# Ten row tiles of a count moved from a dense stage to a gather stage, two PSUM copies moved to VectorE, stores moved to SyncE

## Chip, cores and metric

The kernel runs on one core of a Trainium2 chip. A core has five engines with a queue of instructions each: TensorE (PE in the profile; its weight loads are PEld), VectorE (DVE), ScalarE (ACT), GpSimd (POOL) and SyncE (SP). Each works through its own queue in order and waits on semaphores for the others. The metric is the device time of one execution in microseconds. Times are medians of several runs.

## Reference

Four graph layers follow one another on `x` of 4096 x 256. Each adds its result to `x`, and each starts from `h = relu(layernorm(x))`. The adjacency matrix `adj` is 4096 x 4096 int32 with zeros and ones, about 0.8% ones.

```python
# layer 0: attention over adj, then a dense part for every row
Wh = h @ W                                    # 256 x 256
h_attn = softmax(where(adj > 0, leaky(e_src + e_dst), -9e15)) @ Wh
h_enh = silu(ln(Wh @ fe1_w + fe1_b)) @ fe2_w + fe2_b
B, C, dt = split(Wh @ W_bcdt + b_bcdt, 3)
hs = Wh * ((softmax(dt + A) * B) @ abp_w + abp_b)
h_part, z = split(hs @ W_hz + b_hz, 2)
hs = ((h_part * silu(z) + h_part * D) @ out_w + out_b) * (1 + C @ cp_w + cp_b)
g = sigmoid(silu(ln(concat(h_attn, hs) @ g1_w + g1_b)) @ g2_w + g2_b)
x = x + ln(g * h_attn + (1 - g) * hs + h_enh)
# layer 1: mean over the neighbours, then a projection
a = (adj == 1); deg = a.sum(axis=1)
x = x + (a @ h / deg) @ W.T + b
# layer 2: attention with a leaky logit, elu at the end
# layer 3: attention with Q K^T logits, adj + identity as mask
```

What the change is about is `deg`, the number of ones of each row, which layer 1 divides by, and the dense part of layer 0.

## The kernel before

Rows are cut into 32 tiles of 128 (`NT`), four tiles make a block (`BT`), and there are 8 blocks (`NB`). Each row of `adj` is cut into four quarters of 1024 columns (`NQ`, `QW`). `x` stays on the core in `xs`.

Layer 0's attention loads `adj` as bf16, turns it on PE, codes it and stores the codes to DRAM (`codesT`) for the later layers. Its results are in `xs` and in the projected rows `wh`.

The dense part of layer 0 follows (lines 561 to 798). `dense(b)` is a generator that works one block through all products and yields 30 times. `turn` (L594) transposes four 128 x 128 parts on PE into a PSUM tile of tag `tp`, of which there are three, and has it copied out by the function given: `onto` is a VectorE copy (L602), `nc.scalar.copy` one on ACT (recorded at L599). It is used for `whT` (two halves k = 0 and 1, L661), for `abT` (L703; it lies in a buffer called `kept`, so the profile writes `kept<-tp`), for `comb` (four parts, L754) and for the two `hidden` stages, where ACT evacuates with Silu (L625). `normed` computes row statistics on DVE, a power on POOL (L116), an offset on DVE (L611), and applies both on ACT (L614).

Beside it run the counts. `count(g)` takes one quarter of one row tile (a `[128, 1024]` bf16 tile `a`, loaded by a casting DMA that POOL issues, L639) and runs two ACT instructions over it (L647): the sign of `a - 0.5` and the sign of `a - 1.5`, each summed along the row into `over[:, t, v, q]`. The difference of the two sums, halved, is the number of ones. There are 32 x 4 = 128 such counts and so 256 sign activations. Four `a` buffers (`AHEAD`) are filled three ahead. `with_counts(b)` puts one count behind each of the first 16 steps of `dense(b)`.

`run_staggered(gens, period)` (L29) takes one step of every active generator per tick and starts a new one every `period` ticks, here 16. So the second half of block b runs beside the first half of block b+1, and every tick has one count until the last block is past its sixteenth step. The order in which the program states instructions is not kept exactly: the framework's scheduler may put a ready instruction of later work ahead in its engine's queue.

Layer 1 (L803 to 868) first reduces `over` to `rdeg`, the reciprocal of the degree, for all 32 tiles at once (L837 to 841). `block1(b)` normalizes a block, transposes it and projects it into `v1` (value and rounding rest, so 512 columns). Then `gather(t)` runs for each row tile:

```python
eq = (code == UNIT)                              # DVE, L852, two buffers
for c in range(NT): acc += eq[:, c].T @ v1[:, c] # PE, L856, 32 products, acc has two buffers
lo = acc[:, D:]                                  # ACT, L862
o = (acc[:, :D] + lo) * rdeg[:, t] + b1          # DVE, L864, L865
xs[:, t] += o                                    # DVE, L866
```

The codes come by DMAs of SP (L847) into four buffers. Layer 2 and layer 3 are attentions that read the codes again. In layer 3 each block of two row tiles ends in `weigh3`, which divides, adds `xs` and stores the rows with a DMA issued by POOL (L1109). SP issues the loads of codes of the following row blocks there (`fetch3`, L1006).

Of the kernel before, what the change touches and what calls it, by code (L numbers as in the profile page):

```python
# [21 lines left out]
P = 128  # L22
# [19 lines left out]
def kernel(ctx: ExitStack, tc: tile.TileContext, w: dict, out: bass.AP):  # L42
    nc = tc.nc
    x, adj = w["x"], w["adj"]
    N, D = x.shape
    NT = N // P
    KD = D // P
    BT = 4
    NB = NT // BT
    BW = BT * P  # L50
    QW = 1024
    NQ = N // QW
# [98 lines left out]
    def products(ps, lhsT_of, rhs_of, n):  # L151
        for k in range(n):
            nc.tensor.matmul(  # L153
                out=ps, lhsT=lhsT_of(k), rhs=rhs_of(k), start=(k == 0), stop=(k == n - 1)
            )

# [183 lines left out]
    with ExitStack() as l0:  # L340
# [10 lines left out]
        with ExitStack() as es:  # L351
# [155 lines left out]
            with ExitStack() as ps_:  # L507
# [53 lines left out]
        wp = l0.enter_context(tc.tile_pool(name="l0_w", bufs=1))  # L561
        with ExitStack() as es:
            d = es.enter_context(tc.tile_pool(name="l0_d", bufs=1))
            AHEAD = 4
            code_p = es.enter_context(tc.tile_pool(name="l0_code", bufs=AHEAD))
            small = es.enter_context(tc.tile_pool(name="l0_s", bufs=4))
            pst = es.enter_context(tc.tile_pool(name="l0_pt", bufs=3, space=PSUM))
# [26 lines left out]
            def turn(dst, parts, take):  # L594

                ps = pst.tile([P, BW], F32, tag="tp", name="tp")
                for i, part in enumerate(parts):
                    nc.tensor.transpose(ps[:, ts(i, P)], part, ident)
                take(dst, ps)  # L599
# [30 lines left out]
                        yield  # L630
                return zT

            asked, came = [(t, q) for t in range(NT) for q in range(NQ)], []

            def ask(n):
                for t, q in asked[len(came) : n]:

                    came.append(code_p.tile([P, QW], BF16, tag="a", name="a", bufs=AHEAD))
                    nc.gpsimd.dma_start(out=came[-1], in_=adj[ts(t, P), ts(q, QW)])  # L639

            def count(g):

                ask(g + AHEAD - 1)
                t, q = asked[g]
                for v in range(2):
                    sign = code_p.tile([P, QW], BF16, tag="sign", name="sign", bufs=1)
                    nc.scalar.activation(  # L647
                        sign, came[g], AF.Sign, bias=limits[:, v : v + 1],
                        accum_out=over[:, t, v, q : q + 1],
                    )  # L650

            def dense(b):
                at = ts(b, BT)
# [3 lines left out]
                    out=xt, in_=x[ts(b, BW), :].rearrange("(t p) d -> p t d", p=P)  # L657
# [3 lines left out]
                for k in range(KD):  # L661
                    turn(
                        whT[:, k, :], [wh[:, b * BT + i, ts(k, P)] for i in range(BT)],
                        onto if k else nc.scalar.copy,
                    )
                yield

# [5 lines left out]
                dt = bc[:, :, S : 2 * S]  # L673
# [26 lines left out]
                        yield  # L700
                yield from normed(t1, "fe")
                abT = parts[1, BW][:, 0, :]
                turn(abT, [dt[:, i, :] for i in range(BT)], nc.scalar.copy)  # L703
                yield
                hsT = parts[KD, BW]
                for k in range(KD):
# [81 lines left out]
                nc.gpsimd.tensor_tensor(f, f, xt, ALU.add)  # L788

            def with_counts(b):  # L790
                at, n = b * BT * NQ, BT * NQ
                for k, _ in enumerate(dense(b)):
                    if k < n:
                        count(at + k)
                    yield

            ask(AHEAD - 2)
            run_staggered([with_counts(b) for b in range(NB)], 16)

    with ExitStack() as es:  # L803
        vp = es.enter_context(tc.tile_pool(name="l1_v", bufs=1))
        v1 = vp.tile([P, NT, 2, D], F32R, name="v1")
        w1 = load_matrix(vp, "L1_gnn_WT")
        b1 = load_row(vp, "L1_gnn_b")
        code_p = es.enter_context(tc.tile_pool(name="l1_code", bufs=4))
        eq_p = es.enter_context(tc.tile_pool(name="l1_eq", bufs=2))
        work = es.enter_context(tc.tile_pool(name="l1_work", bufs=2))  # L810
        small = es.enter_context(tc.tile_pool(name="l1_s", bufs=4))
        pst = es.enter_context(tc.tile_pool(name="l1_pst", bufs=2, space=PSUM))
        psm = es.enter_context(tc.tile_pool(name="l1_psm", bufs=3, space=PSUM))
        ps_acc = es.enter_context(tc.tile_pool(name="l1_acc", bufs=2, space=PSUM))

        def block1(b):
            h = work.tile([P, BT, D], F32, tag="h", name="h")
            preln(small, xs[:, ts(b, BT), :], h)
            yield
            hT = transposed_block(work, pst, h, "hT")  # L820
            yield
            for i in range(0, BT, 2):
                ps = psm.tile([P, 2, D], F32, tag="mm", name="mm")
                for u in range(2):
                    products(
                        ps[:, u, :], lambda k: hT[:, k, ts(i + u, P)], lambda k: w1[:, k, :], KD
                    )
                at = slice(b * BT + i, b * BT + i + 2)
                nc.scalar.copy(v1[:, at, 0, :], ps)
                nc.vector.tensor_tensor(  # L830
                    v1[:, at, 1, :], ps, v1[:, at, 0, :].bitcast(F32), ALU.subtract
                )
                yield


        sums = vp.tile([P, NT, 2], F32, name="sums")
        nc.vector.tensor_reduce(sums, over, AX.X, ALU.add)  # L837
        rdeg = vp.tile([P, NT], F32, name="rdeg")
        nc.vector.tensor_tensor(rdeg, sums[:, :, 0], sums[:, :, 1], ALU.subtract)
        nc.vector.tensor_scalar(rdeg, rdeg, 0.5, None, ALU.mult)  # L840
        nc.vector.reciprocal(rdeg, rdeg)
        run_staggered([block1(b) for b in range(NB)], 2)

        def gather(t):
            code = code_p.tile([P, N], BF16, tag="code", name="code")
            for q in range(NQ):
                nc.sync.dma_start(  # L847
                    out=code[:, ts(q, QW)].rearrange("p (c i) -> p c i", i=P),
                    in_=codesT[t // RB][q][:, t % RB, :, :],
                )  # L850
            eq = eq_p.tile([P, N], F32R, tag="eq", name="eq")
            nc.vector.tensor_scalar(eq, code, UNIT, None, ALU.is_equal)  # L852
            yield
            acc = ps_acc.tile([P, 2 * D], F32, tag="acc", name="acc")
            for c in range(NT):
                nc.tensor.matmul(  # L856
                    out=acc, lhsT=eq[:, ts(c, P)], rhs=v1[:, c, :, :],
                    start=(c == 0), stop=(c == NT - 1),
                )
            yield  # L860
            lo = work.tile([P, D], F32, tag="lo", name="lo")
            nc.scalar.copy(lo, acc[:, D : 2 * D])  # L862
# [72 lines left out]
    with ExitStack() as l3:  # L935
# [59 lines left out]
        code_p = l3.enter_context(tc.tile_pool(name="l3_code", bufs=2))  # L995
# [95 lines left out]
        def weigh3(b):  # L1091
            st = rows3[b]
            accs = [ps_acc.tile([P, D + 1], F32, tag="acc", name="acc") for _ in range(RT)]
            for c in range(NT):
                for r in range(RT):
                    nc.tensor.matmul(  # L1096
                        out=accs[r], lhsT=st["y"][:, r, c, :], rhs=v3[:, c, :],
                        start=(c == 0), stop=(c == NT - 1),
                    )
                yield  # L1100
            for r in range(RT):
                t = b * RT + r
                rden = small.tile([P, 1], F32, tag="rden", name="rden")
                nc.vector.reciprocal(rden, accs[r][:, D : D + 1])  # L1104
                o = work.tile([P, D], F32, tag="o", name="o")
                nc.vector.scalar_tensor_tensor(
                    o, accs[r][:, 0:D], rden, xs[:, t, :], ALU.mult, ALU.add
                )
                nc.gpsimd.dma_start(out=out[ts(t, P), :], in_=o)  # L1109

        fetch3(0)
        signs3(0)
# [51 lines left out]
```

## Time and profile before

| what | value |
| --- | --- |
| median of 3 runs | 3056.92 us (3055.16 to 3063.83) |
| the profiled execution's own time | 3058.37 us |
| span of its record | 3056.6 us |
| PE busy | 2874.6 us, 94% |
| DVE busy | 1854.3 us, 61% |
| ACT busy | 1275.1 us, 42% |
| POOL busy | 965.4 us, 32% |
| sign activations (L647) | 256, 1148 ns mean, 293.9 us |
| reading their sums (L647) | 256, 190 ns mean, 48.6 us |
| products of layer 1's sums (L856) | 1024, 239.3 us |
| stores of the result on POOL (L1109) | 32, 542 ns mean |

In the profile a busy time is the time in which an engine had an instruction running. A group is named by line, engine, operation and `out<-in`; "idle before" is how long the engine stood still just ahead of such instructions, with the releaser that ended the wait. The dense part lies between about 624 and 1221 us of the span, layer 1's projections between 1240 and 1286, its sums from there to about 1521.

### The profile page before, as it was taken

The page shows a single profiled execution, that of the slowest core. Times are in us where ns is not written, and L with a number is a line of the kernel's source. Part 1 is how long each engine was busy: PE and PEld are TensorE (multiplying, and loading weights), DVE is VectorE, ACT ScalarE, POOL GpSimd, SP SyncE. Part 2 cuts the span into 40 slices and gives each one's busy share as a digit, 9 for nine tenths or more (in the row PEclk, how much of TensorE's full clock was granted, in tenths as well). Part 3 has the DMA queues.
Part 4 walks back from the last instruction along what each step waited for, and adds up shares of the span by engine and source line. Part 5 has one row for each costly group of instructions (what it writes and reads, how often), then busy time and mean ns, then how long its engine had stood idle before and what let it go on. Part 6 is the DMA issues. An engine that isn't in the chain of part 4 may idle for free.

```text
span 3056.6 us, 34943 instructions
## 1 busy us (share of the span) xinstructions
PE 2874.6 (94%) x13353; PEld 2341.0 (77%) x13353; DVE 1854.3 (61%) x3304; ACT 1275.1 (42%) x1944; POOL 965.4 (32%) x749
## 2 busy tenths in 40 slices
PE   6989999999899999799969999999999999999998
PEld 5778888866555566588758887888888888888887
DVE  5876767335444453544488887745766566566562
ACT  5766555379999963400054434443212111111111
POOL 4676665534454433100026555550000000000000
PEclk9999999999999999899979999999999999999999
DMA  6966655154444420344222222101101101101000
GB/s 143 212 145 126 139 124 154 39 80 76 74 76 75 76 36 7 102 138 141 81 106 79 90 69 83 56 18 59 63 33 61 39 33 61 38 33 61 33 7 8
DMA packets 105745, 234.94 MB, mean 77 GB/s; under 512 B 10701, under 2 KB 27081, under 8 KB 97385
## 3 DMA queue, kind: packets, MB, share of 16 engines
q0 software_dynamic: 39152, 73.04, 15.7%
q1 hardware_dynamic: 63752, 157.04, 14.9%
q10 hardware_dynamic: 2672, 2.62, 0.3%
q8 instruction: 105, 1.72, 0.2%
q14 instruction: 64, 0.52, 0.1%
HBM read 261.96 MB, written 37.81 MB: 98 GB/s over the span
## 4 chain that ended last, share of the span: by engine, by line
issue 26%; PE 17%; DVE 3%; POOL 2%; DMA 1%; ACT 1%; POOLq 0%; DVEq 0%; ACTq 0%
PE acc L325 11%; PE s L153 3%; PE acc L1096 2%; DVE run L237 1%; PE mm L153 1%; DVE y L283 1%; POOL y L287 1%; DMA turned<-codesT 1%; POOL out_dram L1109 1%; ACT y L314 0%; POOL pl_rs L116 0%; ACT hp L889 0%; PE q_ps L153 0%; ACT h L133 0%; DMA ab_row<-l_ab_d 0%
## 5 line engine op out<-in xcount | busy, mean ns | idle before, releaser
L325 PE MATMUL acc<-v,y 128*128 128x257 f32 x4096 | 935.0, 386 | 36.1 <-ACT hp L889 18.5
L325 PEld LDWEIGHTS acc<-v,y 128*128 128x128 f32 x4096 | 776.3, 193 | 151.6 <-ACT hp L889 23.7
L287 POOL TENSOR_TENSOR y<-y,turned 128x1024 f32<-128x1024 f32 (+1 forms) x272 | 550.1, 2037 | 301.5 <-DVE y L283 261.9
L314 ACT ACTIVATE y<-y,sdst 128x512 f32<-128x512 f32 (+1 forms) x544 | 350.7, 689 | 360.7 <-POOL y L287 360.5
L283 DVE SCALAR_TENSOR_TENSOR y<-ab_row,cdst,b 128x512 f32<-128x512 f32 (+1 forms) x544 | 368.6, 711 | 162.5 <-PE acc L325 103.0
L1096 PE MATMUL acc<-v,y 128*128 128x257 f32 x2048 | 454.5, 380 | 0.4 <-DVE rden L1104 0.4
L153 PE MATMUL s<-qT,hT 128*128 128x256 f32 x2048 | 445.2, 379 | 0.7 <-ACT qT L1044 0.7
L153 PEld LDWEIGHTS s<-qT,hT 128*128 128x128 f32 x2048 | 389.2, 190 | 53.9 <-ACT qT L1044 1.4
L1089 ACT ACTIVATE y<-y 128x1024 f32<-128x1024 f32 x128 | 132.2, 1055 | 714.3 <-DVE y L1088 710.0
L1096 PEld LDWEIGHTS acc<-v,y 128*128 128x128 f32 x2048 | 387.4, 190 | 55.6 <-issue 0.8
L237 DVE SCALAR_TENSOR_TENSOR run<-turned,v,run 128x512 f32<-128x512 bf16 (+1 forms) x527 | 379.8, 721 | 58.3 <-DMA turned<-codesT 28.0
L1109 POOL DMA_DIRECT2D out_dram<-o x32 | 17.3, 542 | 933.7 <-DVE rden L1104 932.9
L647 ACT ACTIVATE sign<-a,limits 128x1024 bf16<-128x1024 bf16 x256 | 293.9, 1148 | 18.5 <-DMA a<-in_adj_dram 12.9
L856 PE MATMUL acc<-v,eq 128*128 128x512 f32 x1024 | 239.3, 395 | 0.0
L1058 DVE SCALAR_TENSOR_TENSOR y<-code,s 128x512 f32<-128x512 bf16 x256 | 175.9, 688 | 100.4 <-PE s L153 100.1
L856 PEld LDWEIGHTS acc<-v,eq 128*128 128x128 f32 x1024 | 192.7, 189 | 44.8 <-DVE eq L852 0.3
L1088 DVE TENSOR_TENSOR y<-y,top 128x1024 f32<-128x1024 f32 x128 | 146.2, 1216 | 43.0 <-PE top L1082 43.0
L1065 DVE TENSOR_TENSOR mx<-mx,y 128x512 f32<-128x512 f32 x224 | 154.9, 691 | 7.4
L407 ACT ACTIVATE turned<-cT,log_wide 128x1024 bf16<-128x1024 bf16 x128 | 140.9, 1101 | 32.8 <-PE cT L402 32.5
L153 PE MATMUL mm<-kept 128*128 128x512 f32 x288 | 139.4, 620 | 10.1 <-ACT kept L599 8.6
L852 DVE TENSOR_SCALAR eq<-code 128x4096 fp32r<-128x4096 bf16 x32 | 73.4, 2293 | 114.8 <-PE acc L856 114.8
L153 PE MATMUL mm<-kept,zT 128*128 128x256 f32 x512 | 116.8, 381 | 0.0
(214 smaller groups left out, 2744.0 us busy)
## 6 DMA issues: line engine op xcount, KB each, us to landing
adj_t<-in_adj_dram POOLq DMA_DIRECT2D x128, 256.0 KB, 4.6
codesT<-turned SPq DMA_DIRECT2D x32, 1024.0 KB
a<-in_adj_dram POOLq DMA_DIRECT2D x128, 256.0 KB, 4.2
code<-codesT SPq DMA_DIRECT2D x128, 256.0 KB
turned<-codesT SPq DMA_DIRECT2D x32, 1024.0 KB
code<-codesT SPq DMA_DIRECT2D x64, 512.0 KB
ab_row<-l_ab_d SPq DMA_DIRECT2D x15, 512.0 KB
xt<-in_x_dram SPq DMA_DIRECT2D x8, 512.0 KB
```

Source lines behind the costliest of these rows:

```text
L153: nc.tensor.matmul(out=ps, lhsT=lhsT_of(k), rhs=rhs_of(k), start=(k == 0), stop=(k == n - 1))
L237: nc.vector.scalar_tensor_tensor(st["run"], code, dst, st["run"], ALU.subtract, ALU.min)
L283: nc.vector.scalar_tensor_tensor(y[:, :, k, :], st["ab"][:, 0, :, :], self.cdst[:, c + k : c + k + 1], st["b"], ALU.add, ALU.max,)
L287: nc.gpsimd.tensor_tensor(y, y, mask[:, :, c % QT : c % QT + 2, :], ALU.subtract)
L314: nc.scalar.activation(y[:, :, k, :], y[:, :, k, :], AF.Exp, bias=self.sdst[:, c + k : c + k + 1],)
L325: nc.tensor.matmul(out=acc, lhsT=y[:, r, k, :], rhs=self.v[:, c + k, 0 : D + 1], start=(c + k == 0), stop=(c + k == NT - 1),)
L647: nc.scalar.activation(sign, came[g], AF.Sign, bias=limits[:, v : v + 1], accum_out=over[:, t, v, q : q + 1],)
L856: nc.tensor.matmul(out=acc, lhsT=eq[:, ts(c, P)], rhs=v1[:, c, :, :], start=(c == 0), stop=(c == NT - 1),)
L1058: nc.vector.scalar_tensor_tensor(y[:, :, c : c + 2, :], st["code"][:, :, c : c + 2, :], -BIG / UNIT, ps, ALU.mult, ALU.add,)
L1065: nc.vector.tensor_tensor(mx, mx, y[:, :, c : c + 2, :], ALU.max)
L1088: nc.vector.tensor_tensor(part, part, top, ALU.subtract)
L1096: nc.tensor.matmul(out=accs[r], lhsT=st["y"][:, r, c, :], rhs=v3[:, c, :], start=(c == 0), stop=(c == NT - 1),)
```

## The change

There are three edits. First, only the first 22 row tiles (`COUNTED`) are counted in the dense part: 22 x 4 / 8 = 11 counts per block in the place of 16, behind the first 11 steps of each block. The other ten tiles (40 counts) are counted in `gather(t)`, spread over t = 0 to 27, after `eq` is stated, with four `a` buffers and one `sign` buffer of their own in a new pool. The code of `ask` and `count` becomes the class `Tally`. `rdeg` is computed for tiles 0 to 21 where it was computed for all before, and for each later tile by four small DVE instructions as soon as its four quarters are counted. Second, `whT` for k = 0 and `abT` are copied out of PSUM by DVE (`onto`) in the place of ACT. Third, the result is stored with DMAs that SP issues.

```diff
+    AHEAD = 4
+    COUNTED = 22
+
+    class Tally:
+        def __init__(self, pool, bufs, lo, hi):
+            self.pool, self.bufs = pool, bufs
+            self.asked, self.came = [(t, q) for t in range(lo, hi) for q in range(NQ)], []
+        def ask(self, n):
+            for t, q in self.asked[len(self.came) : n]:
+                self.came.append(
+                    self.pool.tile([P, QW], BF16, tag="a", name="a", bufs=self.bufs)
+                )
+                nc.gpsimd.dma_start(out=self.came[-1], in_=adj[ts(t, P), ts(q, QW)])
+        def count(self, g):
+            self.ask(g + self.bufs - 1)
+            t, q = self.asked[g]
+            for v in range(2):
+                sign = self.pool.tile([P, QW], BF16, tag="sign", name="sign", bufs=1)
+                nc.scalar.activation(
+                    sign, self.came[g], AF.Sign, bias=limits[:, v : v + 1],
+                    accum_out=over[:, t, v, q : q + 1],
+                )
...
+            tally = Tally(code_p, AHEAD, 0, COUNTED)
...
                 for k in range(KD):
                     turn(
                         whT[:, k, :], [wh[:, b * BT + i, ts(k, P)] for i in range(BT)],
-                        onto if k else nc.scalar.copy,
+                        onto,
                     )
...
-                turn(abT, [dt[:, i, :] for i in range(BT)], nc.scalar.copy)
+                turn(abT, [dt[:, i, :] for i in range(BT)], onto)
...
             def with_counts(b):
-                at, n = b * BT * NQ, BT * NQ
+                n = COUNTED * NQ // NB
                 for k, _ in enumerate(dense(b)):
                     if k < n:
-                        count(at + k)
+                        tally.count(b * n + k)
                     yield
...
+        over_a = es.enter_context(tc.tile_pool(name="l1_a", bufs=AHEAD))
...
-        nc.vector.tensor_reduce(sums, over, AX.X, ALU.add)
         rdeg = vp.tile([P, NT], F32, name="rdeg")
-        nc.vector.tensor_tensor(rdeg, sums[:, :, 0], sums[:, :, 1], ALU.subtract)
-        nc.vector.tensor_scalar(rdeg, rdeg, 0.5, None, ALU.mult)
-        nc.vector.reciprocal(rdeg, rdeg)
+
+        def degrees(at):
+            nc.vector.tensor_reduce(sums[:, at, :], over[:, at, :, :], AX.X, ALU.add)
+            nc.vector.tensor_tensor(rdeg[:, at], sums[:, at, 0], sums[:, at, 1], ALU.subtract)
+            nc.vector.tensor_scalar(rdeg[:, at], rdeg[:, at], 0.5, None, ALU.mult)
+            nc.vector.reciprocal(rdeg[:, at], rdeg[:, at])
+
+        tally = Tally(over_a, AHEAD, COUNTED, NT)
+        n_late = (NT - COUNTED) * NQ
+        BESIDE = NT - 4
+        tally.ask(AHEAD - 2)
+        degrees(slice(0, COUNTED))
         run_staggered([block1(b) for b in range(NB)], 2)
...
             nc.vector.tensor_scalar(eq, code, UNIT, None, ALU.is_equal)
+            for g in range(t * n_late // BESIDE, min((t + 1) * n_late // BESIDE, n_late)):
+                tally.count(g)
+                if g % NQ == NQ - 1:
+                    at = COUNTED + g // NQ
+                    degrees(slice(at, at + 1))
             yield
...
-                nc.gpsimd.dma_start(out=out[ts(t, P), :], in_=o)
+                nc.sync.dma_start(out=out[ts(t, P), :], in_=o)
```

More of the change, by code (lines that the diff above doesn't have):

```diff
@@ L563 @@
             d = es.enter_context(tc.tile_pool(name="l0_d", bufs=1))
-            AHEAD = 4
             code_p = es.enter_context(tc.tile_pool(name="l0_code", bufs=AHEAD))
@@ L631, in hidden @@
                 return zT
[L633 to L650, printed above, removed]
+            tally = Tally(code_p, AHEAD, 0, COUNTED)
             def dense(b):
@@ L790, in with_counts @@
             def with_counts(b):
-                at, n = b * BT * NQ, BT * NQ
+                n = COUNTED * NQ // NB
                 for k, _ in enumerate(dense(b)):
                     if k < n:
-                        count(at + k)
+                        tally.count(b * n + k)
                     yield
-            ask(AHEAD - 2)
+            tally.ask(AHEAD - 2)
             run_staggered([with_counts(b) for b in range(NB)], 16)
@@ L836 @@
         sums = vp.tile([P, NT, 2], F32, name="sums")
-        nc.vector.tensor_reduce(sums, over, AX.X, ALU.add)
         rdeg = vp.tile([P, NT], F32, name="rdeg")
-        nc.vector.tensor_tensor(rdeg, sums[:, :, 0], sums[:, :, 1], ALU.subtract)
-        nc.vector.tensor_scalar(rdeg, rdeg, 0.5, None, ALU.mult)
-        nc.vector.reciprocal(rdeg, rdeg)
+        def degrees(at):
[6 more added lines that the diff above has]
+        BESIDE = NT - 4
+        tally.ask(AHEAD - 2)
+        degrees(slice(0, COUNTED))
         run_staggered([block1(b) for b in range(NB)], 2)
```

## Prediction

> **What bounds the kernel now.** I read the page first. TensorE (PE) is busy 94% of the span, so a change can only help where PE waits or runs at a lower clock. In the page's forty slices ACT shows 9 tenths only in the stretch near 620 to 1115 us: the dense part of layer 0, whose `sign` activations count the ones of the adjacency matrix. So I asked for the busy time by windows. I cut them at PE's own marks: 623.90 is the first transpose of the dense part, 677.96 and 1123.83 are the starts of the `bc` products of blocks 1 and 7, 1220.90 is the last dense product. Columns: stretch, length, busy us of each engine (instructions), granted clock, DMA share, GB/s.
>
> ```profile
> core 0: us, PE busy (x) PEld busy (x) DVE busy (x) ACT busy (x) POOL busy (x), PEclk, DMA share, GB/s
> 623.90:677.96 54.06, 48.37 (x185) 30.80 (x184) 20.62 (x44) 47.95 (x79) 23.86 (x28) 0.97 0.61 94
> 677.96:1123.83 445.87, 417.36 (x1539) 265.96 (x1538) 209.76 (x422) 405.00 (x646) 210.25 (x200) 0.97 0.47 73
> 1123.83:1220.90 97.07, 91.90 (x330) 57.64 (x328) 43.36 (x87) 28.13 (x40) 32.58 (x19) 0.96 0.02 6
> 1240.36:1285.56 45.20, 42.05 (x202) 34.38 (x203) 29.58 (x86) 28.45 (x54) 7.04 (x7) 0.91 0.38 124
> 1285.56:1521.90 236.34, 235.98 (x1016) 191.10 (x1014) 108.15 (x124) 12.50 (x33) 0.06 (x1) 1.00 0.39 116
> ```
>
> In the six block periods from 677.96 to 1123.83 PE is idle 445.87 - 417.36 = 28.5 us and ACT is busy 91%. In layer 1's sums (last row) PE never stops and ACT does 12.5 us of work in 236. Next, PE's own waits in those six periods (total, times, longest):
>
> ```profile
> PE tp L598 <- ACT whT L599: 16.0, 4, 5.0
> PE mm L153 <- ACT kept L599: 7.8, 6, 2.1
> PE tp L598 <- ACT t L614: 2.8, 4, 1.7
> PE tp L598 <- DVE whT L602: 1.4, 4, 0.3
> PE mm L153 <- DVE kept L709: 0.5, 2, 0.3
> ```
>
> They sum to 28.5, all of the idle time, and 26.6 of it ends on ACT. The two largest are the two ACT copies that the diff touches: `whT` k=0 (line 664) and `abT` (line 703, an alias of a `kept` buffer). Why these 0.56 us copies are late shows in ACT's timeline around one of them:
>
> ```profile
> 972.41 1.15 ACT L647 ACTIVATE sign<-a,limits 128x1024 bf16<-128x1024 bf16 x1
> 973.47 0.19 ACT L647 ACTIVATION_READ_ACCUMULATOR sign<-a,limits 128x1 f32 x1
> 975.57 1.15 ACT L647 ACTIVATE sign<-a,limits 128x1024 bf16<-128x1024 bf16 x1 [1.91 <-DMA a<-in_adj_dram]
> ...
> 977.99 0.56 ACT L599 COPY whT<-tp 128x512 f32<-128x512 f32 x1
> 978.45 0.59 ACT L599 COPY comb<-tp 128x512 f32<-128x512 f32 x1
> ```
>
> and PE beside it:
>
> ```profile
> 972.92 0.66 PE L598 MATMUL tp<-ident,xs 128*128 128x128 f32 x4 [0.35 <-DVE whT L602]
> 978.61 1.97 PE L598 MATMUL tp<-ident,hs 128*128 128x128 f32 x8 [5.03 <-ACT whT L599]
> 980.37 4.53 PE L153 MATMUL mm<-bcw,whT 128*128 128x257 f32 x16
> ```
>
> The transposes of `whT` were done by 972.1. The copy stood in ACT's queue behind signs, one of them waiting for its DMA; its PSUM buffer (three of tag `tp`) stayed taken, and the fifth transpose group of the chain found none free.
>
> **What the Trainium skill says.** "TensorE: Matmul & The Clock Gate", What's actually happening: PE falls to half clock after about one idle window of 3.4 us and needs as long a busy window to recover. The trace agrees: the eight transposes above took 1.97 us after a 5.03 us gap (1.09 for the same eight at 1122.89 without a gap), the sixteen products 4.53 (3.64 at 1123.83). "ScalarE: Activation LUTs", What ACT_TABLE_LOAD costs: about 1283 ns for each switch of table; the trace has 15 loads of 1283 ns for eight blocks and none at a sign, so layer 1 pays for one load at most. "SBUF — State Buffer", SBUF: two separate sides: a VectorE instruction in a two-port mode shuts GpSimd out of writing DMA descriptors while it runs; in layer 1 `eq` is such a candidate, 2.29 us of each 7.4. No record here shows a GpSimd DMA beside it. "DMA: Bandwidth & Descriptors", SWDGE vs HWDGE vs iDMA: a casting DMA must be GpSimd's, a plain one may be SyncE's. That fits the diff: the adjacency loads stay on POOL, only the store moves.
>
> **The change part by part.**
>
> *Counts out of the dense part.* 40 of 128 counts leave, 80 signs. The signs above start 1.28 us apart, so ACT loses 80 x 1.28 = 102 us. Per block: 16 x 2 x 1.28 = 41 becomes 11 x 2.55 = 28 us. ACT's other work per block, from the rows of the dense window (8 zT at 0.78, 8 t at 0.80, 4 xs at 0.59, 4 sz at 0.69, whT, abT, two comb, exp, tanh, two table loads), is about 23 us. So a period asks 64 us of ACT before and 50 after. PE's floor for a period is what it needed when no sign was left: 1121.07 to 1189.13, 68.1 us. Before, the average period was 445.87 / 6 = 74.3. The excess is 37.5 us over six periods: 28.5 of idle and 9 of slow clock after the gaps. That is the most that this stretch can give.
>
> *whT k=0 to DVE.* The wait of 16.0 goes: DVE is 47% busy, and around 972 it has only `hs` evacuations at 0.48 each. The copy costs 0.69 there (the row of `whT` by DVE) against 0.56. Both whT copies are then one after the other on DVE (1.4 us), beside 1.8 us of `xs` and `hs` transposes; I put 1 us in all for short waits. Late next would be the comb copies on ACT; they come after ticks 11 to 15 of the block's period, which have no counts now, so ACT's queue should be short. Saved: 15.
>
> *abT to DVE.* Of 7.8 I let only 2 go. The copy no longer waits behind signs, but at that place DVE holds the last `t2` evacuation, its statistics (0.69 + 0.69 + 0.18 + 0.17) and then waits about 1.15 us for POOL's power before `gl_off`. Depending on whether the copy lies ahead of or behind that wait, abT is ready some 0.5 us earlier to 1.7 us later than by ACT (six periods: 3 saved to 10 lost; at best all 7.8 goes).
>
> *The rest of the stretch.* Of the 2.8 of `t` I take 2, since ACT is less behind; of the 9 of slow clock 6.5, as the long gaps go and some of those beside abT stay. At the start (5.7 us of gaps up to 677.96) the 3.4 us behind `bc` hangs on an exp behind the first signs, which are still there: 0.5. Sum for the dense part: 15 + 2 + 2 + 6.5 + 0.5 = 26 us. POOL waits 122 us there for signs to free `a` buffers; less of it is a by-product I count at nothing.
>
> *Counts into layer 1.* 80 signs in 236 us are 102 + 12.5 = 115 us for ACT, hidden under PE's sums. Per tile (7.38 us) it is 1.43 counts, 3.7 us, and `lo` 0.37. DMA: 15,843 packets in the window 680 to 1110 took 45.6% of 430 us for 110 loads, 1.8 us each, so 1.43 x 1.8 = 2.6 us of 7.38, 35%; with 41% for codes 76%, under saturation, and codes run up to four tiles ahead. DVE gets ten times four small instructions (0.17 to 0.4 each) and up to a wait for ACT's last sign; behind it stands the next `eq`, which has 3.8 us of slack (it waits that long for PE). Cost 0; if the cover is gone, see the rival below. The 22-row reduction at the start replaces the 32-row one (0.42 + 1.98 + 0.18 + 0.35): nothing either way.
>
> *Layer 1's projections, 1240 to 1286.* Here PE is the bound with 3 us of gaps and ACT is busy 63%. Signs whose data has come may fall between the copies that PE needs, 1.28 us each, and two to three extra POOL issues (0.56) stand beside the powers. Bounds 0 to 8; I take 3 lost. Below zero is excluded, since nothing is removed there.
>
> *The store.* 32 issues leave POOL, which is otherwise idle in layer 3. SP's queue holds the stores ahead of later fetches, but a fetch is needed a whole row block (57.8 us) later. Only the last counts: the two issues on POOL take 1.14 us; between 0.5 lost and 1.5 gained, 1 taken.
>
> Sum: -26 + 3 + 0 - 1 = -24. The profiled execution took 3058.4 (span 3056.6), which gives 3034; it lies 1.5 above the median of 3056.9, so 3032.5 on the median's scale.
>
> **The rivals.** What a measurement of this kernel can tell from no change is about 0.3%, 9 us.
>
> *More is freed.* The whole 37.5 and some of the start's 5.7 goes, and layer 1 loses nothing: about -39, 3018. For it: every wait but 1.9 us ends on ACT. Against it: abT's new place.
>
> *The bubble moves.* abT and the comb copies become what PE waits for, with slow clock behind them; whT's 16 goes but 6 to 8 comes back, and layer 1's projections lose 6: about -11, 3046. For it: comb 0 and 2 stay on ACT, and in the ticks that still have counts ACT asks as much as before. Against: the ticks ahead of comb are free.
>
> *Slower: signs ahead of `lo` in layer 1.* ACT works in order, and the instruction order is laid out by a scheduler, not by the loop alone (PE's record shows products of the sums placed among the projections). If it puts the 40 counts early, between few `lo`, then each `lo` waits for several counts, the two PSUM accumulators stay full, and PE stops. With k tiles sharing all counts the loss is 102 - 7.0 k - 7.4 us. From k below 8, over five counts a tile, the loss passes 40 and eats the gain; at k = 6 it is 53, giving 3080. For it: only four `a` buffers and their DMAs hold the counts back. Against: 28 ticks are laid out in the loop, and the dense part's signs stayed within about two counts of their ticks.
>
> *It doesn't do what it says*: layer 1's loads starve and the counts finish late, with the gain given back in full: 3057.
>
> **How the numbers follow.** Likeliest case 0.58 (3020 to 3045), more freed 0.12, bubble moves 0.18, slower 0.10, no effect 0.02. Predicted time 3032. The range 3014 to 3056 takes in the two neighbours and leaves out the slower one. Faster than 3047.7: 0.56 + 0.12 + 0.09 = 0.77; within 0.3%: 0.02 + 0.08 + 0.02 = 0.12; slower 0.11.
>
> **What would show it.** PE's waits in the dense part no longer name `whT` by ACT; the six periods are near 70 us; the eight `hs` transposes take 1.1 us everywhere. abT's wait is seen as `kept` by DVE L602, near 1 us a period. In the sums PE stays without gaps at 7.38 us a tile with ACT near half busy. Wrong it would be if waits on `comb` by ACT or on `acc` by `lo` appear, or if 1240 to 1286 grows by over 8 us.

## Result and the profile after

The kernel after takes 3038.74 us (3034.09 to 3042.76, 4 runs), against 3057.93 (3055.16 to 3063.83, 4 runs) for the kernel before on the same chip: a ratio of 0.9934, 95% interval [0.9912, 0.9957]. That is 0.66% faster. The forecast was 3032 (3014 to 3056), faster. The side is right and the size is near. Where the time went is not as forecast.

The profiled execution took 3034.09 us, its span is 3032.3, 24.3 below the span before. Both traces were cut at the same marks of PE:

| stretch | before, us | after, us | difference | predicted |
| --- | --- | --- | --- | --- |
| start of the dense part to `bc` of block 1 | 54.1 | 54.5 | +0.5 | −0.5 |
| six block periods | 445.9 | 437.8 | −8.1 | −25.5, with the next row |
| last `bc` to the last dense product | 97.1 | 99.0 | +1.9 | (above) |
| gap ahead of layer 1's first transpose | 19.5 | 15.0 | −4.5 | none |
| layer 1's projections | 45.6 | 47.8 | +2.2 | +3 |
| layer 1's sums | 235.6 | 237.5 | +1.9 | 0 |
| gap ahead of layer 2's first transpose | 12.4 | 0.96 | −11.4 | none |
| layer 2 | 586.6 | 588.0 | +1.4 | none |
| last DVE instruction to the end | 10.5 | 2.8 | −7.7 | −1 |

Layer 3 takes 925.6 us in both; the start of the dense part came 0.5 earlier. The stretch that should give 26 gives under 6. Two layer boundaries give 16, and the end 7.7.

Busy time by windows of the kernel after, with the six periods one by one (columns as before: stretch, length, busy us of each engine with its instructions, granted clock, DMA share, GB/s):

```profile
core 0: us, PE busy (x) PEld busy (x) DVE busy (x) ACT busy (x) POOL busy (x), PEclk, DMA share, GB/s
...
677.92:746.42 68.50, 67.35 (x250) 42.35 (x249) 34.56 (x71) 65.52 (x104) 32.43 (x32) 1.00 0.49 73
746.42:819.66 73.24, 68.52 (x259) 43.12 (x257) 36.39 (x73) 69.23 (x111) 36.07 (x35) 1.00 0.52 80
819.66:894.51 74.85, 70.09 (x258) 44.43 (x257) 35.29 (x73) 69.42 (x111) 36.07 (x35) 0.98 0.52 78
894.51:976.88 82.37, 70.64 (x259) 44.74 (x257) 47.74 (x115) 56.15 (x89) 39.57 (x33) 0.94 0.32 52
976.88:1047.13 70.25, 69.53 (x257) 44.67 (x257) 35.97 (x81) 21.45 (x30) 22.61 (x15) 0.98 0.02 8
1047.13:1115.67 68.54, 67.82 (x259) 43.30 (x257) 36.75 (x82) 21.45 (x30) 25.19 (x16) 1.00 0.03 8
...
1229.62:1277.04 47.42, 43.19 (x199) 35.41 (x199) 21.78 (x41) 39.43 (x76) 11.26 (x15) 0.86 0.70 186
1277.04:1514.70 237.66, 237.66 (x1020) 191.07 (x1018) 130.62 (x234) 95.30 (x171) 28.41 (x35) 1.00 0.59 151
```

Read the ACT column downwards. It is not 50 in each of six periods, as I had worked out, but 65 to 69 in three, 56 in the fourth, and 21 in the last two. The counts are not eleven a period: of sign activations, the same windows of that tile hold 75, 81, 81, 58, 0 and 0 records, two for each. About 40 signs a period run, until none is left. The instruction order has them so: the loop states 22 a block, and the scheduler puts ready ones of later blocks ahead. It was so before, too, where the loop states 32 a block: 74 to 86 records in each of the first five periods and 62 in the sixth, in which the signs run out. There the last sign starts ahead of the `bc` of block 7, up to which the loop has stated 113 of the 128 counts:

```profile
1114.12 1.13 ACT L647 ACTIVATE sign<-a,limits 128x1024 bf16<-128x1024 bf16 x1
1123.83 3.64 PE L153 MATMUL mm<-bcw,whT 128*128 128x257 f32 x16
```

That the counts run ahead could have been read from the trace before. In the kernel after, DVE has 115 instructions in the fourth row where the third has 73.

PE's waits in these six periods (total us, times, longest):

```profile
PE tp L624 <- DVE whT L628: 9.6, 3, 8.3
PE tp L624 <- ACT comb L625: 7.3, 3, 2.6
PE tp L624 <- ACT t L640: 4.6, 5, 1.8
PE tp L624 <- ACT zT L651: 2.0, 4, 0.5
```

`whT` by ACT (16.0) and `kept` by ACT (7.8) are gone. In their place stand `comb` by ACT, in the periods where ACT is full, and one single wait of 8.3 on a `whT` that DVE copies. DVE's timeline ahead of that one:

```profile
967.96 0.47 DVE L756 SCALAR_TENSOR_TENSOR hs<-mm,gain,obc 128x256 f32<-128x256 f32 x1
...
969.62 2.29 DVE L131 SCALAR_TENSOR_TENSOR pl_off<-pl_mv,pl_rs 128x4 f32<-128x4 f32 x1 [0.66 <-POOL pl_rs L116]
971.83 0.41 DVE L121 BATCH_NORM_STATS2 pl_st<-xs 128x6 f32<-128x256 f32 x1
...
972.68 0.48 DVE L756 SCALAR_TENSOR_TENSOR hs<-mm,gain,obc 128x256 f32<-128x256 f32 x1
973.08 0.16 DVE L114 TENSOR_SCALAR pl_ve<-pl_mv 128x4 f32<-128x4 f32 x1
974.37 0.16 DVE L131 SCALAR_TENSOR_TENSOR pl_off<-pl_mv,pl_rs 128x4 f32<-128x4 f32 x1 [1.13 <-POOL pl_rs L116]
974.44 0.87 DVE L756 SCALAR_TENSOR_TENSOR hs<-mm,gain,obc 128x256 f32<-128x256 f32 x2
975.23 1.28 DVE L628 COPY whT<-tp 128x512 f32<-128x512 f32 x2
```

Every `pl_` line is layer 1: the statistics of blocks that the dense part has already finished, some 260 us ahead of layer 1's first transpose. They wait for POOL's powers, and `hs` and `whT`, which PE needs, wait behind them in DVE's order. One `pl_off` takes 2.29 us for 128 x 4 elements; the next one takes 0.16. Beside the long one POOL runs a `tensor_tensor` of 2.34 us from 969.55. The Trainium skill, "SBUF — State Buffer", section on the two separate sides, says that a VectorE instruction with two SBUF inputs and a GpSimd one that reads SBUF exclude each other for a whole instruction; these two records agree: the long `pl_off` starts 0.07 us behind POOL's instruction and ends with it, at 971.9.

The end of the program: the instructions of the line behind the last store, by the queue that runs them (durations in ns: least, median, longest; then first and last start in us), before and then after:

```profile
L1160 POOLq DRAIN  x3: 46/93/9454, 3046.4 to 3056.3; - x3
```

```profile
L1183 POOLq DRAIN  x3: 46/93/8322, 2077.2 to 3031.8; - x3
```

At the end each queue drains and meets the others. POOL's first drain takes 9.45 us before and starts at 3046.4, behind its last store: 10.5 us of tail. After, POOL has nothing to do in layer 3, its drain starts at 2077.2, and its 8.32 us are over 940 us before the end.

### The profile page after: what moved, and what is told of

Same layout as the page of the kernel before. It is cut to its first block, busy times and chain, and to the rows that moved or that the text cites. A ratio compares the mean times of both kernels' runs of the same rounds, so it can differ in the third digit from the quotient of the medians.

```text
span 3032.3 us, 35001 instructions
## 1 busy us (share of the span) xinstructions
PE 2874.8 (95%) x13353; PEld 2338.8 (77%) x13353; DVE 1873.0 (62%) x3360; ACT 1266.3 (42%) x1928; POOL 955.8 (32%) x717
## 5 line engine op out<-in xcount | busy, mean ns | idle before, releaser
L179 ACT ACTIVATE sign<-a,limits 128x1024 bf16<-128x1024 bf16 x256 | 294.0, 1148 | 18.4 <-DMA a<-in_adj_dram 12.4
L172 POOL DMA_DIRECT2D a<-in_adj_dram x128 | 78.3, 613 | 186.6 <-ACT sign L179 145.1
L870 DVE TENSOR_SCALAR eq<-code 128x4096 fp32r<-128x4096 bf16 x32 | 73.5, 2296 | 86.8 <-PE acc L879 79.9
```

What stands on the lines that cost most here:

```text
L179: nc.scalar.activation(sign, self.came[g], AF.Sign, bias=limits[:, v : v + 1], accum_out=over[:, t, v, q : q + 1],)
```

## The experiments

Each kernel has a letter for the theory it is to try: A, the end of the program depends on who stores; B, the new pool moves addresses, and what may run early at the layer boundaries changes with them; C, with the copies on DVE the bubble moves to `comb` on ACT; D, the counts that run ahead keep ACT full; E, layer 1's statistics that run ahead cost the dense part; F, what moving the 40 counts is worth by itself. Ratios are to the kernel before on the same chip.

**Store alone (A).** The kernel before with one edit:

```diff
-                nc.gpsimd.dma_start(out=out[ts(t, P), :], in_=o)
+                nc.sync.dma_start(out=out[ts(t, P), :], in_=o)
```

> The kernel before with the third edit alone: SP stores the result. Theory A (found in the two traces: from the last VectorE instruction to the span's end it is 11.0 us before and 3.3 after): the store by POOL costs about 7.7 us at the end of the program, so this kernel is 7 to 8 us faster than before, with the end 3.3 us behind the last VectorE instruction. Rival (the prediction's step): about 1 us, between 0.5 lost and 1.5 gained, and the 7.7 us belong to something else.

Measured: 3048.65 us, ratio 0.997 [0.9962, 0.9979]. The tail is 2.7 us, where it was 10.5; everything ahead of it lies within 3 us of before. The longest POOL drain starts at 2091.2 here and takes 8.32 us, so the store is worth 7.8 us, all of it by letting that drain end early.

**Addresses alone (B).** The kernel before with an unused pool of the new pool's size in layer 1:

```diff
         eq_p = es.enter_context(tc.tile_pool(name="l1_eq", bufs=2))
+        pad_p = es.enter_context(tc.tile_pool(name="l1_pad", bufs=1))
+        for k in range(5):
+            pad = pad_p.tile([P, QW], BF16, tag=f"pad{k}", name="pad")
+            nc.gpsimd.memset(pad[:, 0:2], 0.0)
```

> The kernel before with nothing but a pool of five buffers of 2 KB per partition in layer 1, at the place where the change has its new pool; each buffer gets a two-column memset and is not used. Theory B: the new pool moves layer 1's later buffers, so that layer 2's first normalization no longer waits for memory that layer 1 frees at its end; PE's gap between layer 1's sums and layer 2 falls from 12.4 us to 1 or 2, and layer 1's own start shortens by some 4 us; together 12 to 18 us faster than before with no edit of the work. Rival: the shorter gaps come from the moved counts or from VectorE's order of work, and this kernel is within 3 us of before, with the 12.4 us gap still there.

Measured: 3056.42 us, ratio 0.9989 [0.998, 0.9999]. The two gaps are 14.97 and 0.96, those of the kernel after to 0.01 us. But the stretch behind the last `bc` takes 108.1 (97.1 before) and layer 2 592.2 (586.6). PE at the start of layer 2, first before, then with the unused pool (in brackets PE's idle time and what ended it):

```profile
1533.94 2.17 PE L144 MATMUL tp<-ident,h 128*128 128x128 f32 x8 [12.40 <-ACT h L133]
```

```profile
1526.52 2.30 PE L144 MATMUL tp<-ident,h 128*128 128x128 f32 x9 [0.96 <-ACT h L133]
```

And PE's largest wait behind the last `bc` in this kernel:

```profile
PE tp L598 <- DVE whT L602: 8.0, 1, 8.0
```

Ten kilobytes of each partition that nothing reads give 16 us at two places and take 16.6 back at two others. The boundaries of the kernel after are therefore not an effect of counting. Before, layer 2's statistics all run after the last tile of the sums (the first at 1523.42); with the unused pool they run beside the sums, from 1298.7 on, and in the kernel after from 1369.5 on, once its last sign is done. A part of the short boundary comes back at once: layer 2's first product then waits for `w` by DVE, 4.8 us here and 3.0 in the kernel after, a wait that isn't there before. The half of theory B that expected a net gain fell.

Layer 1's statistics are let in early in the same way. Before, the first starts at 1235.8, behind the last dense block. With the unused pool it starts at once behind the last sign, whose sum is read from 1115.3 to 1115.5:

```profile
1115.52 0.75 DVE L121 BATCH_NORM_STATS2 pl_st<-xs 128x6 f32<-128x256 f32 x2 [2.31 <-ACT sign L647]
```

So with this pool the statistics may start when the counts of the dense part are through, and the earlier these end, the deeper in the dense part that is: the last sign ends at 950.6 in the kernel after, and the first statistics start at 955.2. That their buffers then lie where the counts had theirs is inferred from this wait; the traces show no addresses.

**Copies alone (C).** The kernel before with `whT` k = 0 and `abT` copied by DVE:

```diff
-                        onto if k else nc.scalar.copy,
+                        onto,
...
-                turn(abT, [dt[:, i, :] for i in range(BT)], nc.scalar.copy)
+                turn(abT, [dt[:, i, :] for i in range(BT)], onto)
```

> The kernel before with the second edit alone: whT k=0 and abT are copied by VectorE. Theory C: ACT stays saturated with 16 counts a block, so PE's waits move from whT to the comb copies and the hidden evacuations on ACT; the six periods keep an average of 72 to 75 us (74.3 before) and the kernel is within 8 us of before. Rival (the prediction's step): the 16 us of waits on whT go, and the six periods lose 12 to 20 us together.

Measured: 3053.6 us, ratio 0.9989 [0.9982, 0.9997]; the six periods take 440.0, 6 less than before, but only 3 less than in the two kernels above (443.4 and 443.2), whose dense part is that of before. PE's waits there:

```profile
PE tp L598 <- ACT comb L599: 13.0, 4, 5.1
PE tp L598 <- ACT t L614: 8.6, 10, 3.0
PE tp L598 <- ACT zT L625: 2.6, 5, 0.8
```

Of 23.8 us that went with `whT` and `kept`, 13.0 came back on `comb`, and `t` rose by 5.8. The bubble moved, as one of the recorded rivals has it.

**Counts held to their block (D).** The kernel after, where each block's signs take their bias from a tile that the block itself writes, so that none can start earlier:

```diff
-        def count(self, g):
+        def count(self, g, limits=limits):
...
+                pace[b] = small.tile([P, 2], F32, tag="pace", name="pace")
+                nc.vector.scalar_tensor_tensor(
+                    pace[b], gain[:, 0:2, 0], 0.0, limits, ALU.mult, ALU.add
+                )
...
-                    if k < n:
-                        tally.count(b * n + k)
+                    if 1 <= k <= n:
+                        tally.count(b * n + k - 1, pace[b])
```

> The changed kernel with the counts of each block held to that block: the sign's bias is a small tile that VectorE makes anew from each block's gain, so that the scheduler cannot place signs of later blocks ahead. Theory D: in the changed kernel the counts ran ahead, 16 or more a period until they were used up in the fifth period, so ACT stayed saturated there; held to 11 a period all six periods come to 68 to 70 us (73.0 on average in the changed kernel, sum 438), 18 to 25 us faster than the changed kernel. Rival: the excess comes from VectorE's new copies and their order, and pacing leaves the periods at 72 to 75 us, the time within 5 us of the changed kernel.

Measured: 3042.89 us, ratio 0.9952 [0.9937, 0.9967]. The 18 to 25 us below the kernel after that I expected didn't come: the intervals of the two ratios overlap. The periods are 69.0, then 71.8 to 72.0, with exactly 22 signs in each: 428.5 in all, 9.3 below the kernel after, but the stretch behind loses more. The waits on `comb` and `whT` are gone, but `t` has 15.5. That stretch takes 112.5 (99.0 in the kernel after), with 9.1 on `hs` by DVE: there layer 1's statistics now run, from 1171.7 on, behind the last sign's end at 1165.6. Why `t` is late, from POOL's timeline:

```profile
1130.11 0.53 POOL L172 DMA_DIRECT2D a<-in_adj_dram  x1 [1.49 <-ACT sign L179]
1132.65 0.53 POOL L172 DMA_DIRECT2D a<-in_adj_dram  x1 [2.02 <-ACT sign L179]
1135.19 0.53 POOL L172 DMA_DIRECT2D a<-in_adj_dram  x1 [2.02 <-ACT sign L179]
1135.74 1.03 POOL L116 TENSOR_TENSOR fe_rs<-fe_ve,mhalf 128x4 f32<-128x4 f32 x1
```

and DVE's:

```profile
1132.07 0.17 DVE L114 TENSOR_SCALAR fe_ve<-fe_mv 128x4 f32<-128x4 f32 x1
1136.81 0.16 DVE L637 SCALAR_TENSOR_TENSOR fe_off<-fe_mv,fe_rs 128x4 f32<-128x4 f32 x1 [4.57 <-POOL fe_rs L116]
```

The power's input is ready at 1132.2; the power starts at 1135.7, behind loads whose buffers wait for signs. I had counted POOL's waits for `a` buffers at nothing. Spread evenly, the counts, with the tile that holds them, cost every period some 3.8 us (71.9 against the floor of 68.1), and clustered they cost only the periods that have them.

**Counts without the other two edits.** The kernel after, with both copies on ACT and the store on POOL as before:

```diff
-                        onto,
+                        onto if k else nc.scalar.copy,
...
-                turn(abT, [dt[:, i, :] for i in range(BT)], onto)
+                turn(abT, [dt[:, i, :] for i in range(BT)], nc.scalar.copy)
...
-                nc.sync.dma_start(out=out[ts(t, P), :], in_=o)
+                nc.gpsimd.dma_start(out=out[ts(t, P), :], in_=o)
```

> The changed kernel with the copies back on ACT and the store back on POOL: the first edit alone. Theory: the last gap of the program is 10.5 us again (2.8 in the changed kernel); the layer boundaries stay short (15 and 1 us), since the new pool is there; in the dense part whT waits on ACT return while the counts last, four to five periods at 73 to 78 us, then two near 69. Time 9 to 15 us above the changed kernel. Rival: the copies were worth 16 us on their own, and the six periods go back to the 446 us of before.

Measured: 3049.6 us, ratio 0.9974 [0.9963, 0.9984]; six periods 441.4, tail 10.5, gaps and layer 1 as in the kernel after. PE waits 12.5 on `whT` by ACT and 10.3 on `whT` by DVE (longest 8.9). So the copies are worth 441.4 - 437.8 = 3.6 us in the dense part, little more than the 2.7 by which kernels with the same dense part differ there, and the store 7.7. The long wait on a `whT` by DVE is there without the new copies.

**The new pool placed last (B).** The kernel after with one line moved:

```diff
-        over_a = es.enter_context(tc.tile_pool(name="l1_a", bufs=AHEAD))
...
         small = es.enter_context(tc.tile_pool(name="l1_s", bufs=4))
+        over_a = es.enter_context(tc.tile_pool(name="l1_a", bufs=AHEAD))
```

> The changed kernel with the new pool of layer 1 placed behind all others of its layer, so that the buffers of work and small lie where they lay before. Theory B: the short boundaries are owed to the addresses: layer 1's first gap goes back from 15.0 to about 19.5 us and layer 2's from 1.0 to about 12.4, while the 8.3 us gap in the fifth period, where layer 1's statistics ran ahead on VectorE, disappears; in sum about 5 to 10 us slower than the changed kernel. Rival: the boundaries keep their 15 and 1 us, so they come from the moved counts.

Measured: 3030.34 us, ratio 0.9914 [0.9897, 0.993]. Both gaps are back (19.39 and 11.01), as expected, and layer 1's statistics start at 1217.8, though the last sign of the dense part ends at 951.1. But the kernel is not slower than the kernel after, as I had expected; its median is 8 us lower, in another set of runs, and the ratios' intervals overlap. The six periods take 425.1, and PE waits for no `whT` there. Between the two traces the dense part gains 13.0 and the two boundaries lose 14.5; the sums (233.2) and layer 2 (583.6) are 4.3 and 4.4 shorter, so 5.5 are left. The early statistics cost the dense part about what their short boundaries bring.

**A gate (E).** The kernel after, where layer 1's statistics may be gathered only once the last dense block's tanh is done:

```diff
+    gate = const.tile([P, BT, 2], F32, name="gate")
...
-    def preln(small, xb, h):
+    def preln(small, xb, h, after=None):
...
+        if after is not None:
+            nc.vector.tensor_copy(mv, after)
...
                 nc.scalar.activation(f, f, AF.Tanh, scale=0.5)
+                if b == NB - 1:
+                    nc.vector.tensor_scalar(gate, f[:, :, 0:2], 0.0, None, ALU.mult)
...
-            preln(small, xs[:, ts(b, BT), :], h)
+            preln(small, xs[:, ts(b, BT), :], h, gate)
```

> The changed kernel in which layer 1's statistics can't start before the last dense block's tanh: their result tile is first written from a small tile that VectorE makes there. Theory E: the 8.3 us gap on whT by DVE in the fifth period is made by statistics of layer 1 that ran ahead on VectorE and POOL and held up hs; with the gate the fifth period falls from 82.4 to 74 or below; layer 1's first gap stays between 15 and 19.5; in sum 4 to 9 us faster than the changed kernel. Rival: the gap is owed to VectorE's new copies and stays.

Measured: 3021.81 us (3019.75 to 3023.89, 4 runs), ratio 0.9882 [0.9867, 0.9897], the lowest of all: 17 us below the kernel after, with intervals apart, where 4 to 9 were expected. The two traces are only 10.2 us apart (spans 3022.1 and 3032.3), so they don't show where the rest of the 17 lies. Its periods by windows:

```profile
747.10:820.50 73.40, 70.09 (x258) 44.25 (x257) 35.69 (x73) 69.32 (x110) 36.03 (x35) 0.98 0.51 80
820.50:896.00 75.50, 69.95 (x259) 43.90 (x257) 36.22 (x73) 69.40 (x111) 36.08 (x35) 0.98 0.49 77
896.00:969.40 73.40, 68.55 (x259) 43.14 (x258) 37.77 (x79) 55.91 (x90) 31.76 (x27) 1.00 0.36 58
969.40:1037.20 67.80, 67.73 (x259) 43.27 (x257) 36.55 (x73) 21.39 (x31) 25.53 (x16) 1.00 0.03 8
```

The fourth period has 79 DVE instructions where the kernel after has 115, and takes 73.4 where that takes 82.4; the fifth is at 67.8 with PE busy throughout. In sum the six periods take 426.5, 11.3 less. Both copies are still on DVE, so the rival, that they make the 8.3 us gap, falls. The waits on `comb` (7.1) stay. The gap ahead of layer 1 grows to 16.6 (+1.7), that of layer 2 stays at 0.96. The sums fall to 234.0 (-3.5), which I did not look into.

**Gate and pacing together (D on top of E).** The kernel with the gate, and the pace tile as above, but written by two ACT instructions with scale 0:

```diff
+                for v in range(2):
+                    nc.scalar.activation(
+                        pace[b][:, v : v + 1], gain[:, v, :], AF.Identity,
+                        scale=0.0, bias=limits[:, v : v + 1],
+                    )
```

> Gate and pacing together; the bias that paces is made by ACT, since VectorE's two-input instruction took 1.9 us beside POOL's. Theory D and E: six periods at 69 to 72 us (sum 415 to 430), the stretch from the last bc to the dense part's end near 98 us (112.5 in the paced kernel without a gate), L1's gap 15 to 19.5: 12 to 22 us faster than the changed kernel and the fastest of all. Rival: PE's waits on t by ACT (15.5 us in the paced kernel), which come from POOL's powers queued behind adjacency loads, stay or grow, and the kernel is within 8 us of the changed one.

Measured: 3025.38 us (3019.78 to 3030.33), ratio 0.9893 [0.9876, 0.991]; six periods 427.0, against 426.5 with the gate alone. The fastest of all, as I had expected it to be, it is not: pacing adds nothing to the gate. That the counts run ahead is not in itself a loss, once nothing else runs ahead behind them: three periods at 73 to 76 and three at 67.8 to 68.5 cost as much as six near 71. With the tile written by ACT an evenly loaded period takes 70.8.

**The move itself (F).** The kernel with the gate, with all 128 counts back in the dense part and layer 1's new pool filled with unused buffers:

```diff
-    COUNTED = 22
+    COUNTED = 32
...
         over_a = es.enter_context(tc.tile_pool(name="l1_a", bufs=AHEAD))
+        for k in range(AHEAD + 1):
+            pad = over_a.tile([P, QW], BF16, tag=f"pad{k}", name="pad", bufs=1)
+            nc.gpsimd.memset(pad[:, 0:2], 0.0)
```

> The kernel with the gate, but all 32 row tiles are counted in the dense part (16 counts a block) and none in layer 1, whose new pool is kept full by unused buffers; both copies stay on VectorE and the store on SyncE. What is left of the change to compare is the move of the 40 counts alone. Theory F (the move is worth what ACT's saturation in periods 5 and 6 costs, less what it adds in layer 1): the six periods take 436 to 442 us in the place of 426.5, PE's waits on comb by ACT rise from 7 to about 13, the projections and sums fall by 3 to 5; in all 3026 to 3032, so 5 to 10 slower than with the move. Rival (the move is worth nothing once the copies are on VectorE and the statistics are held back): the six periods below 430 and the time within 3 us of the gate kernel's, or below it.

Measured: 3038.32 us, ratio 0.9928 [0.9906, 0.995]. The periods are 68.9, 76.1, 75.5, 73.6, 73.6 and 73.5, in sum 441.2, and PE waits for:

```profile
PE tp L627 <- ACT comb L628: 12.5, 4, 4.9
PE tp L627 <- ACT t L643: 8.2, 11, 3.0
PE tp L627 <- ACT zT L654: 2.5, 4, 0.8
```

So, with the gate, moving 40 counts is worth 14.7 us in the six periods, all that the two spans differ by, and about 16 in the medians, 3038.32 against 3021.81 (measured in different sets of runs; the ratios' intervals do not meet). The rival, that it is worth nothing, falls. The direction was expected, the gain was larger than the 5 to 10 I gave. The projections (46.0 and 47.3) and the sums (235.4 and 234.0) differ by little over 1 us either way: layer 1's price all but vanishes. With the gate and none of the counts moved, the kernel is as fast as the whole change without a gate (ratios 0.9928 and 0.9934).

**The last ACT copies (C on top of E).** The kernel with the gate, and `comb` copied by DVE throughout:

```diff
-                        onto if k % 2 else nc.scalar.copy,
+                        onto,
```

> The kernel with the gate, and the two comb copies that are still on ACT copied by VectorE as well. Theory (the 7.1 us that PE waits on comb by ACT, and the slow clock behind them, are gone): the six periods take 416 to 421 us in the place of 426.5, and the time is 5 to 9 below the gate kernel's, 3013 to 3017. Rival (the bubble moves once more): PE waits as long on t or zT by ACT, or on comb by DVE, whose four copies of 0.69 us in a row are now later than the transposes; the six periods at 424 or more and the time within 3 us of the gate kernel's.

Measured: 3025.95 us (3021.63 to 3029.57), ratio 0.9889 [0.9868, 0.991], no better than the gate alone; six periods 429.5.

```profile
PE tp L627 <- ACT t L643: 13.4, 13, 3.9
PE tp L627 <- ACT zT L654: 0.5, 1, 0.5
```

`comb` is gone from the list and `t` has risen from 5.9 to 13.4. The rival is right: in a period in which ACT has 69 us of work, taking a copy from it moves the wait to its next customer.

## Why the prediction was right in size and wrong in its parts

- **Counts out of the dense part: the step that failed.** "Per block: 16 x 2 x 1.28 = 41 becomes 11 x 2.55 = 28 us" took the loop's places for the program's. "The dense part's signs stayed within about two counts of their ticks" misread the trace before, where they are 15 counts ahead at block 7's `bc`. ACT's work does fall by 102 us (405 to 303 in the six periods), but in the last 2½ of them and not by 13 in each. "The excess is 37.5" stood as the ceiling of the stretch; the move reaches 14.7 of it, shown by the pair of kernels with the gate.
- **`whT` to DVE, "saved: 15".** The wait of 16.0 did go. "ACT's queue should be short" at `comb` was false in the full periods: 7.3 came back (13.0 with all counts in place), and with both copies' gain at 3 to 6 us the 15 is out of reach. The rival "bubble moves" named it, at 0.18, and by the prediction's own sign, "Wrong it would be if waits on `comb` by ACT" appear, this part was wrong.
- **`abT`, 2 of 7.8.** PE waits for no `kept` in the six periods after, so the whole 7.8 of waiting went; what the copy is worth alone was not measured.
- **The rest of the dense part, 9 us.** DVE was taken to have room for the copies, by its load of 47%. What is ahead of a copy in its order matters, and that was statistics of another layer: 8.3 in one wait. The gate shows their price: 11.3 in the six periods. That counts which finish early let them in was in no rival.
- **Layer 1's sums, cost 0.** They cost 1.9. The scheduler put the 40 counts early here too, all before 1370, about three beside each `lo`. PE kept running. Three a tile is under the five that the slower rival asks for. That rival's own numbers don't come out of its formula: the loss eats the forecast gain of 24 already at k = 10 (24.6), not below 8, and at k = 6 the loss of 53 gives 3032 + 53 = 3085, not 3080.
- **Projections, +3.** Measured +2.2.
- **The store, 1.** The mechanism was misplaced, not only the size: I compared the issue times (1.14 us on POOL), and the 7.7 lies in POOL's drain behind them.
- **Not in the sum at all:** -16 at the two boundaries, from where the new pool lies. The same pool let the statistics in that cost the dense part 11.3.

Terms of -20 too much in the dense part, and of -7 and -16 left out, nearly cancel. That the total came so near was luck. The side was right for recorded reasons that were half right: the counts and the waits on ACT were worth moving, and the rest came from elsewhere.

## What to carry to other kernels

Before a loop's spread is turned into a load per period, count the records per period in the trace: work that depends on nothing runs as early as its buffers allow, in one lump. Ask next what its absence lets run ahead, and hold that back with a true dependence if it stands in a critical engine's queue; here the gate took off 17 us more in the medians (10 between the traces), where the whole change had taken 19. And a new buffer pool is a change by itself: an unused one of the same size, in the kernel before, shows what it does.

## What the hardware showed unasked

- A final store issued by POOL made the end 7.7 us longer than one by SP: 10.5 to 10.6 in the four profiles with POOL's store, 2.6 to 2.9 in the others. What takes its drain 8.3 to 9.5 us stays open; that it may be had early, once POOL's work is done, is shown.
- A two-input DVE instruction on 128 x 4 elements takes 0.16 us at the median and 2.31 at the longest in the kernel after, 0.16 at the longest before; the two long ones (2.29 and 2.31) each run beside a `tensor_tensor` of POOL of 2.34 to 2.35.
- After the 8.29 us gap the eight `hs` transposes took 1.91 us (1.04 to 1.18 in three other periods of that kernel), with a granted clock of 0.50 from 976.8 to 980.0. This agrees with the half clock after an idle window that the Trainium skill gives, "TensorE: Matmul & The Clock Gate", What's actually happening.
- Layer 2's length ranges from 583.6 to 592.2 us over kernels that do not touch it. It goes with the layout of layer 1's pools (583.6 to 586.8 with the new pool last or without it, 587.8 to 592.2 with it ahead of the others), but was not taken apart.
